# A graph layer on one core: early filter loads into empty tiles, and the four distance products of a pair as one step of TensorE

## The chip, the cores and the metric

The kernel runs on one core of a Trainium2 chip. TensorE (PE in the profile) multiplies matrices, with weight loads listed apart (PEld); VectorE (DVE), ScalarE (ACT) and GpSimd (POOL) work on elements; SyncE (SP) issues most DMAs. SBUF is the memory on the core, PSUM the accumulator banks that TensorE writes. The metric is the device time of one launch, in microseconds.

## What is computed

The input `x` is (64, 256, 256): 64 graphs of 256 nodes with 256 features; `adj` is a 0/1 matrix per graph. Everything is float32. Cut to what matters:

```python
h = maximum(layernorm(x), 0)
# branch 1: two convolutions along the nodes, 1 tap and 17 taps
c = relu(bn1(conv1d(h.T, conv1_w)))
x_conv = relu(bn2(conv1d(c, conv2_w, pad=8)) + h.T).T
# branch 2: messages weighted by distance in a space of 3 numbers
s = h @ w_se.T + b_se                        # (64, 256, 3)
dist = sq[:, :, None] + sq[:, None, :] - 2 * s @ s.T   # sq = sum(s * s)
A = exp(-dist) * adj
x_nmp = A @ relu(h @ w_msg.T + b_msg)
# a GRU cell on both
gi = concat([x_conv, x_nmp]) @ w_ih.T + b_ih
gh = h @ w_hh.T + b_hh
r, z = sigmoid(gi_r + gh_r), sigmoid(gi_z + gh_z)
n = tanh(gi_n + r * gh_n)
out = x + (1 - z) * n + z * h
```

## The kernel before

**Tiling.** Two graphs make a pair (index `i`, 32 pairs), four pairs make a batch (index `b`, 8 batches). The 17-tap convolution is done for a whole batch in a transformed domain. VectorE makes the transform of the input, TensorE multiplies each of 16 bins with that bin's transformed filters, VectorE transforms back (`branch_back` to `p_back`). Each bin has up to three filter matrices ("kinds"), 47 in all, each 128x2x256 numbers (256 KB). They are computed once at the start (`filter_steps`), written to DRAM tensors `filt`, and fetched again for every batch.

**Filters in a batch.** `pending` is the list of filters still to be fetched, `free` the list of free slots. There are nine slots in SBUF (`wb`). `load_kinds` (L902) takes a slot from `free` and a filter from `pending` and issues the DMA on SP. `product` (L927) multiplies with the filter at the head, puts its slot back into `free` and calls `load_kinds`. `begin(m)` (L938) does the first kind of two bins into an accumulator tile `acc` and has ScalarE copy it to the tile's second bank; `complete(m)` (L945) adds the other kinds. Between the transforms of two batches the same nine slots serve the GRU: `roles` (L1071) names them, and `give` (L1077) returns them. Seven are returned at the end of a batch, the last two (`tz0`, `tz1`) inside the next.

**A pair.** `message` computes the messages and the three numbers `s`, `embed` transposes these into `zT`. `affinity` (L1018) computes the distances: for each graph and half, four times in all, a product of nine rows from `zT`, at rows 0, 32, 64 and 96, into one of four PSUM banks (`aux`, a ring), then the exponential on ScalarE, then the multiplication with `adj` on VectorE. `aggregate` multiplies with the messages into a tile `xnm` (a ring of two). `gates` (L1178) does the GRU of a pair with a seven-product scheme: `seven` (L1152) opens two `acc` tiles and one `aux` bank, and calls sums on VectorE (`wb` tiles named by role, weights `w_x`, `w_ih`, `w_hh`). `finish` and `deliver` bring the result out. From the fifth pair on, rows of `adj` and of `h` are turned by transposing DMAs: `load_adj` (L630) fetches turned rows into `adjh` by four DMAs, `join_adj` (L640) is ScalarE's two copies from `adjh` to the tile that VectorE reads.

**What sets the order.** The code doesn't issue instructions. `Recorder` takes each call as a task with an engine, an assumed cost and its dependences (`record`, L334); `plan` (L388) is a list scheduler that simulates the engines with these costs, with TensorE's tasks due in the order of the recording, and `emit` (L463) issues all tasks in the planned order. Each engine then works through its list in order, and waits where an operand isn't there. Almost everything after the first batch's start is one plan. All instructions are issued by one line of `record`, so the profile shows L371 for nearly all; the tile names tell them apart. In the profile, `V`, `U`, `Sv`, `PT` hold transforms, `Yv` the transformed-back result.

The end of a batch, where the next batch's filters are asked for, and the two slots returned inside it, read:

```python
        if b + 1 < NB:
            pending.extend(TURNS)

        def between():
            join_adj(nxt)
        gates(i + 3, between)
        message(nxt)
        if b == NB - 1:
            finish(NP - 1)
        give("axn", "axc", "ah")
        give("bh", "bxn", "bxc", "e")
        load_kinds()
```

## Time and profile before

| | us |
|---|---|
| median of 3 runs (lowest to highest) | 1692.25 (1688.8 to 1693.15) |
| profiled execution, its own time | 1694.44 |
| span in that profile | 1692.7 |
| TensorE busy | 1662.7 |
| VectorE busy | 1458.6 |
| ScalarE busy | 1133.6 |
| GpSimd busy | 227.9 |
| TensorE waiting for filter DMAs, whole span | 5.3 |
| matmuls of the distance products: instructions, busy | 256, 31.0 |

The profile is of one execution. An engine's busy time says how much it did, not whether it set the end; the chain that ended last and the waits of TensorE say that. A wait `A <- B` in the view of waits means that engine A stood idle until B had finished; a wait for several things is put down to the one that came last. In the timeline each line is a start, a length, an engine, an operation with its tiles as out<-in, and a count; the tile's buffer numbers are left out. A float32 matmul appears as two MATMUL instructions.

### The profile page before, as it was taken

Reading aid. Unit: us, or ns where it says so; the run is one execution under the profiler, and the core shown is the slowest. Engines: PE = TensorE matmul, PEld = TensorE weight load, DVE = VectorE, ACT = ScalarE, POOL = GpSimd, SP = SyncE. Lnnn points to the kernel's source line nnn. Section 1 sums busy time; section 2 is a strip of 40 time slices with the busy share of each in tenths; the row PEclk is TensorE's granted clock in tenths of the full one; section 3 lists DMA queues with packets and bytes.
Section 4 is the critical chain, followed back from the end, with each engine's and each line's share of the span. In section 5 each row is a group of like instructions: output and inputs, shape, how many; then the busy total and the mean of one; then the engine's idle time right before and its main releaser. Section 6 shows DMA issues by size and latency. Waiting matters only on the chain.

```text
span 1692.7 us, 26271 instructions
## 1 busy us (share of the span) xinstructions
PE 1662.7 (98%) x8984; PEld 1420.2 (84%) x8984; DVE 1458.6 (86%) x3401; ACT 1133.6 (67%) x2029; POOL 227.9 (13%) x245
## 2 busy tenths in 40 slices
PE   9999999999999999999999999999999999999997
PEld 6888878988889788888889887898888978898886
DVE  7978989798898998898988988979988989789545
ACT  5545776686767767677665877578576776667554
POOL 4211010022010121102110031002211022000010
PEclk9999999999999999999999999999999999999999
DMA  9981566856568365784458645684646846376032
GB/s 240 304 275 61 128 123 160 276 138 128 111 199 235 94 131 112 229 210 97 116 119 270 166 97 117 159 270 111 142 109 204 225 100 131 82 237 144 13 58 55
DMA packets 314936, 261.37 MB, mean 154 GB/s; under 512 B 192875, under 2 KB 240263, under 8 KB 314802
## 3 DMA queue, kind: packets, MB, share of 16 engines
q1 hardware_dynamic: 297010, 216.71, 48.5%
q0 software_dynamic: 17376, 42.66, 11.2%
q8 instruction: 71, 1.16, 0.3%
q14 instruction: 63, 0.52, 0.1%
q10 hardware_dynamic: 416, 0.32, 0.1%
HBM read 156.60 MB, written 43.78 MB: 118 GB/s over the span
## 4 chain that ended last, share of the span: by engine, by line
PE 64%; DVE 29%; DMA 4%; issue 2%; ACT 2%; SPq 0%; DVEq 0%; ACTq 0%
PE acc L371 44%; PE aux L371 20%; DVE V L371 6%; DVE T L371 4%; DVE tr L371 4%; DVE U L371 3%; DVE wb L371 3%; DMA wb<-filt 3%; DVE gn L371 2%; DVE acc L371 2%; DVE Yv L371 1%; DVE PT L371 1%; DVE st L371 1%; DVE msg L371 1%; DMA hh<-halves 1%
## 5 line engine op out<-in xcount | busy, mean ns | idle before, releaser
L371 PE MATMUL acc<-wb,w_ih 128*128 128x256 f32 x768 | 191.9, 379 | 0.0
L371 PEld LDWEIGHTS acc<-wb,w_ih 128*128 128x128 f32 x768 | 146.0, 190 | 19.7
L371 POOL DMA_DIRECT2D back<-in_x_dram x62 | 56.8, 1056 | 750.8 <-ACT back L371 717.5
L371 POOL TENSOR_TENSOR rstd<-rstd,neg_half 128x4 f32<-128x4 f32 x32 | 84.8, 2650 | 455.4 <-DVE shift L371 266.4
L371 PE MATMUL aux<-wb,w_x 128*128 128x256 f32 x576 | 139.9, 384 | 2.5 <-ACT e L371 2.3
L371 PE MATMUL acc<-wb,w_x 128*128 128x256 f32 x576 | 136.2, 382 | 5.3 <-DVE acc L371 5.3
L371 DVE SCALAR_TENSOR_TENSOR V<-T,V 128x128 f32<-128x128 f32 (+2 forms) x448 | 139.9, 372 | 0.0
L371 ACT COPY back<-tr 128x512 uint16<-128x512 uint16 x124 | 128.0, 1077 | 15.2 <-DVE tr L371 14.9
L371 PEld LDWEIGHTS acc<-wb,w_x 128*128 128x128 f32 x576 | 108.0, 190 | 30.5 <-DVE acc L371 12.3
L371 PEld LDWEIGHTS aux<-wb,w_x 128*128 128x128 f32 x576 | 108.8, 191 | 22.1 <-ACT e L371 4.3
L371 PE MATMUL aux<-w_msg,hT 128*128 128x259 f32 x512 | 121.5, 381 | 0.0
L371 PEld LDWEIGHTS acc<-U,wb 128*128 128x128 f32 x1024 | 117.1, 192 | 2.9 <-DMA wb<-filt 1.1
L371 PE MATMUL acc<-U,wb 128*128 128x128 f32 x1024 | 117.6, 275 | 1.6 <-DMA wb<-filt 0.9
L371 PE MATMUL acc<-V,wb 128*128 128x128 f32 x1024 | 118.6, 275 | 0.0
L371 PEld LDWEIGHTS acc<-V,wb 128*128 128x128 f32 x1024 | 116.4, 192 | 0.7 <-DMA wb<-filt 0.3
L371 PE MATMUL acc<-wb,w_hh 128*128 128x256 f32 x384 | 110.1, 381 | 0.7 <-ACT acc L371 0.7
L371 ACT ACTIVATE gn<-acc,bn_columns 128x512 f32<-128x512 f32 (+1 forms) x64 | 43.5, 680 | 97.2 <-PE acc L371 85.6
L371 PEld LDWEIGHTS aux<-w_msg,hT 128*128 128x128 f32 x512 | 96.5, 190 | 14.2
L371 PE MATMUL acc<-Yv,w_ih 128*128 128x256 f32 x380 | 107.9, 379 | 0.1
L371 PE MATMUL aux<-hT,w_c 128*128 128x512 f32 x224 | 105.5, 593 | 0.8 <-DVE msg L371 0.8
L371 PE MATMUL aux<-e,msg 128*128 128x256 f32 x448 | 103.6, 380 | 0.0
L371 PE MATMUL acc<-hT,w_hh 128*128 128x256 f32 x380 | 103.5, 381 | 0.0
(196 smaller groups left out, 3885.6 us busy)
## 6 DMA issues: line engine op xcount, KB each, us to landing
wb<-filt SPq DMA_DIRECT2D x376, 256.0 KB
back<-in_x_dram POOLq DMA_DIRECT2D x62, 256.0 KB, 5.4
out_dram<-back POOLq DMA_DIRECT2D x62, 256.0 KB, 2.8
x<-in_x_dram SPq DMA_DIRECT2D x58, 256.0 KB
halves_d<-halves SPq DMA_DIRECT2D x28, 512.0 KB
adjh<-halves_d SPq DMA_DIRECT2D x112, 128.0 KB
hh<-halves SPq DMA_DIRECT2D x108, 128.0 KB
filt<-Yv SPq DMA_DIRECT2D x18, 224.0 KB
```

Of the source, the lines that this page charges most:

```text
L371: self.tasks.append(Task(engine, lambda: method(*args, **kw), cost, size, self.first))
```

## The change

Four things are different.

- `affinity` takes its four `aux` banks first, then records its four products as one task of TensorE (`joined`): the scheduler can put nothing between them. The four exponentials follow. A task now holds a list of calls, and `emit` makes all of them.
- The assumed cost of such a small product in the scheduler is 0.155 instead of 0.23. The costs of a joined task are added.
- In the last `between` of each batch but the last, after `join_adj(nxt)`, four further slots are added: two in `adjh`, whose content has just been copied, and two in the `xnm` tile that isn't in use. `load_kinds` is called at once, so four filters of the next batch are asked for before the gates of the last pair end.
- `product` doesn't return these four slots to `free`; they serve once per batch.

Since one plan orders everything, a changed task or cost can also move instructions elsewhere. In the built program the orders of all five engines differ in places; the instructions are the same but for the two tiles that four filters in each of seven batches go to.

```diff
@@ record
-                cost = 0.23
+                cost = 0.155
...
-        k = len(self.tasks)
-        self.tasks.append(Task(engine, lambda: method(*args, **kw), cost, size, self.first))
+        if self.joined is not None and engine == "tensor":
+            k = self.joined
+            if k == len(self.tasks):
+                self.tasks.append(Task(engine, [], 0.0, 0, self.first))
+            self.tasks[k].call.append(lambda: method(*args, **kw))
+            self.tasks[k].cost += cost
+        else:
+            k = len(self.tasks)
+            self.tasks.append(Task(engine, [lambda: method(*args, **kw)], cost, size, self.first))
@@ emit
-            self.tasks[k].call()
+            for call in self.tasks[k].call:
+                call()
@@ product
-        free.append(k)
+        if k < SLOTS:
+            free.append(k)
         load_kinds(2)
@@ affinity
-        for g in range(G):
-            for c in range(MC):
-                q = g * MC + c
-                p = aux()
-                rows_q = slice(q * Q, q * Q + KD)
-                mm(p[:, :N], ZT[rows_q, :P], ZT[rows_q, P:], start=True, stop=True)
-                nc.scalar.activation(e_tile[:, g, c], p[:, :N], AF.Exp, scale=-1.0)
+        ps = [aux() for _ in range(G * MC)]
+        nc.joined = len(nc.tasks)
+        for q, p in enumerate(ps):
+            rows_q = slice(q * Q, q * Q + KD)
+            mm(p[:, :N], ZT[rows_q, :P], ZT[rows_q, P:], start=True, stop=True)
+        nc.joined = None
+        for q, p in enumerate(ps):
+            nc.scalar.activation(e_tile[:, q // MC, q % MC], p[:, :N], AF.Exp, scale=-1.0)
@@ end of a batch
         def between():
             join_adj(nxt)
+            if b + 1 < NB:
+                spare = [adjh.bitcast(FP).rearrange("p a n -> p (a n)").rearrange("p (k c d) -> p k c d", k=2, c=DC)[:, k]
+                         for k in range(2)]
+                t = xnms.tiles[(xnms.n + 1) % 2].rearrange("p c (k d) -> p (c k) d", d=D)
+                spare += [t[:, k * DC:(k + 1) * DC] for k in range(2)]
+                slots[SLOTS:] = spare
+                free.extend(range(SLOTS, SLOTS + len(spare)))
+                load_kinds()
         gates(i + 3, between)
```

## Prediction

> **What bounds the kernel now.** First the page: busy shares and the chain that ended last.

> ```profile
> span 1692.7 us, 26271 instructions
> ...
> PE 1662.7 (98%) x8984; PEld 1420.2 (84%) x8984; DVE 1458.6 (86%) x3401; ACT 1133.6 (67%) x2029; POOL 227.9 (13%) x245
> ...
> PE acc L371 44%; PE aux L371 20%; DVE V L371 6%; DVE T L371 4%; DVE tr L371 4%; DVE U L371 3%; DVE wb L371 3%; DMA wb<-filt 3%; DVE gn L371 2%; DVE acc L371 2%; DVE Yv L371 1%; DVE PT L371 1%; DVE st L371 1%; DVE msg L371 1%; DMA hh<-halves 1%
> ```

> TensorE is busy 98% of the span and carries most of the chain. Only work taken off TensorE, or a wait or a slow clock on TensorE itself, can move the end. Next, the products that read zT (the distances), in the timeline of TensorE; columns are start, length, instruction and count. A float32 matmul is two instructions here.

> ```profile
> 135.56 0.69 PE L371 MATMUL aux<-zT 9*128 9x256 f32 x2
> 136.18 0.49 PE L371 MATMUL acc<-PT,wb 128*128 128x128 f32 x2
> 136.60 0.69 PE L371 MATMUL aux<-zT 9*128 9x256 f32 x2
> 137.22 0.49 PE L371 MATMUL acc<-PT,wb 128*128 128x128 f32 x2
> 137.64 0.69 PE L371 MATMUL aux<-zT 9*128 9x256 f32 x2
> 138.26 0.61 PE L371 MATMUL acc<-PT,wb 128*128 128x128 f32 x2
> 138.80 1.22 PE L371 MATMUL aux<-zT 9*128 9x256 f32 x2
> ...
> 910.28 0.71 PE L371 MATMUL aux<-zT 9*128 9x256 f32 x8
> ```

> One product alone holds TensorE 0.62 us (135.56 to 136.18); four in a row take 0.65 us together (910.28 to the next matmul at 910.93). Going through all 32 pairs of graphs, 27 already have the four in a row. Five don't: the pairs at 89.2 and 135.6 (one by one), at 303.6/309.8 and 563.4/570.2 (in two parts) and at 1558.4 to 1570.0 (in three or four). Third, windows of TensorE's clock (columns as on the page; the tenth figure is the granted clock):

> ```profile
> 138.50:145.33 6.83, 6.83 (x29) 5.96 (x29) 3.99 (x8) 2.81 (x6) 1.13 (x2) 0.50 0.24 77
> 145.40:152.00 6.60, 6.60 (x36) 5.90 (x35) 4.88 (x12) 3.91 (x9) 0.00 (x0) 1.00 0.00 0
> ...
> 1561.86:1565.27 3.41, 3.41 (x9) 2.45 (x8) 3.26 (x8) 1.69 (x5) 0.45 (x1) 0.50 0.22 82
> ```

> Twice after the start-up the clock is halved, both times just behind distance products that stand apart. Fourth, the waits of TensorE from 296 to 1520 us, and the start of one batch of the transform in the timeline:

> ```profile
> PE acc L371 <- DMA wb<-filt: 4.4, 7, 1.3
> PE acc L371 <- DVE acc L371: 3.3, 6, 1.1
> PE aux L371 <- ACT e L371: 2.3, 5, 0.5
> ...
> 1092.13 8.40 SPq L371 DMA_DIRECT2D wb<-filt  x10
> 1095.83 1.05 PE L371 MATMUL acc<-Sv,wb 128*128 128x128 f32 x8
> 1098.13 2.94 PE L371 MATMUL acc<-Sv,wb 128*128 128x128 f32 x24 [1.25 <-DMA wb<-filt]
> ```

> The filters of a batch are issued only 4 to 5 us before its first product, since their slots hold the sums of the last gates until then; TensorE did two filters and stood 1.25 us for the third.

> [...] The four products use rows from 0, 32, 64 and 96[...]: 0.65 us for four against 0.62 for one. [...] Here 256 KB took 2.8 to 5.8 us from issue to last arrival at the start of a batch (arrival of each transfer's semaphore in the trace, batch at 892 us).

> **The change, part by part.** The sum is made against the profiled execution: 1694.44 us, 1.74 more than its span.

> 1. Joined products. In 27 pairs nothing changes on TensorE. At 89.2 and 135.6: 4 x 0.62 = 2.50 becomes 0.65, -1.85 each. At 303.6 and 563.4: 0.63 + 0.63 becomes 0.65, -0.62 each. At the end: the stall before 1558.43 stays in another guise, since the next matmul needs Yv, which ScalarE delivers at 1559.7; the third and fourth products (0.62 each) and the 0.68 us wait before the third, less 0.65 for the joined step: -1.3. Sum -6.2. The joined step asks for all four aux banks at once; at 89.2 the last of the four was emptied at 88.8 (ScalarE's copy of taps 88.24 + 0.58), so no wait there. Behind the step on TensorE stand products that don't need its result; the four exponentials take 1.21 us in a row on ScalarE (910.97), as they already do in 27 pairs.

> 2. The clock. If the scattered products caused the two half-clock stretches, joining them removes 6.83/2 = 3.4 and 3.41/2 = 1.7 us. No grouped step is followed by one. Between 0 and 5.1; I take 4.3: the first whole, half of the second, because a TensorE stall of about 2 us for Yv remains there.

> 3. Early filters. In each of seven batches four filter loads (256 KB) go into adjh and the idle xnm tile during the gates before; the first four products find them in place, and the seven slots that come free at the old moment serve products 5 to 11, 3.6 us later (four products of 0.9 us). The waits above sum to 4.4 us. Of these 1.0 (at 896.75) has a second cause: ScalarE's copy out of the accumulator ended at 896.52. So -3.5; between 0 and -5, the latter if waits put down to ScalarE's zT (0.7) are filters too. The order of the built program shows these loads on SP ahead of the last transposes, among the hh loads.

> 4. What moves. The adjacency rows (4 x 128 KB) that stood before the batch now follow it on SP: two behind the eleventh filter, two behind the 33rd, and wait for the first products to free adjh. In the trace of before the 33rd filter was issued at 920.16, 28 us into the batch; transfers around it took 3 to 6 us. The ScalarE copy that needs them is put behind the accumulator copy of the fifth pair of bins (925.46 before), so it may start late by at most 0.5 us; behind it stands the copy at 927.25, whose reader on TensorE comes after eight w_msg products that end at 934.2. Hidden by about 5 us; without that cover 1.4 us a batch. SP's transpose of hh (4.2 us of issue) stands behind the two loads and comes 1.3 us later; it landed at 926.75 and its next reader was issued at 931.13. GpSimd only swaps a small multiply with a load.

> 5. New order. The list is replanned with 0.155 us a product (joined 0.62, measured 0.65) where it had 0.23. In the gates one or two w_x products move from before a distance step to behind it. The stall there (0.4 us, for e's bank) turns into one for VectorE's sum in acc, due at the same time (971.38 against 971.40 in the trace): nothing. VectorE is 91 to 93% busy in the gates, so not every microsecond taken off TensorE is kept. No row prices that: between 0 and 8 us; I take 2.5.

> Sum: -6.2 - 4.3 - 3.5 + 2.5 = -11.5: the profiled execution would take 1683. The median of the runs shown, 1692.25, is 2.2 below the profiled one, so I predict 1692.25 - 11.5 = 1681 for the median.

> **Rivals.**

> - *Little but the joining counts.* The products were together in 27 of 32 pairs, the clock falls again elsewhere, and the first product of a batch is held by the accumulator anyway (896.52 above). Then -6.2 with 1 to 2 us given back: about 1687.5. Against it: at 1098.13 no accumulator was waited for.
> - *All of it is kept.* Both clock stretches and all filter waits go, nothing is given back: -6.2 - 5.1 - 5 = -16.3: 1676. For it: TensorE has only 30 us idle, and VectorE waits on TensorE more often than the reverse.
> - *Slower: the late adjacency rows.* SP issues in order, and ScalarE works in order: if the second pair of rows lands more than about 10 us after its issue at some 920.6, ScalarE's copy holds the accumulator copy past 934 and TensorE stands. To end 0.3% slower than before it must eat the other gains of 11.5 and 5.1 more, 16.6/7 = 2.4 us a batch, so it decides from a landing some 12 us after issue: about 1698. Against it: transfers there took 3 to 6 us, and the queue has room (261 GB/s over that stretch of 50 us, while the first filters landed 0.65 us apart, some 400).

> **How the numbers follow.** 0.3% (5.1 us) is about what a measurement of this kernel can tell from no change. Forecast, 1677 to 1687: 0.55. All kept: 0.13, faster too. Joining alone: 0.20, of which 0.12 is below 1687.2 and 0.08 within the bound. Late rows or another new stall of that size: 0.12, of which 0.10 slower. So faster 0.80, same 0.10, slower 0.10. Range 1673 to 1691: the low end takes all gains with some reserve, the high end joining alone with its gain mostly given back.

> **What would show it.** Right: 32 groups of eight zT instructions, no half clock at 138 and 1562, waits of TensorE for filters from 4.4 us to below 1, the first four filters landed before a batch starts. Wrong: waits of ScalarE for adjh or of TensorE for its copies inside the batch; waits for acc from VectorE that grow from 3.3 us to 10 or more; half clock in a new place.

## The result, and the profile after

The changed kernel took 1670.33 us in the median (1669.41 to 1671.88), the kernel before 1692.13 (1688.8 to 1693.15): a ratio of 0.9877 [0.9861, 0.9893]. That is 21.8 us less, about twice the forecast 11.5 us and below the range of 1673 to 1691. Its profiled execution took 1671.88 us, with a span of 1670.1. First its page: span, busy shares, and the chain that ended last.

```profile
span 1670.1 us, 26281 instructions
...
PE 1645.7 (99%) x8984; PEld 1413.3 (85%) x8984; DVE 1456.8 (87%) x3401; ACT 1127.2 (67%) x2029; POOL 236.0 (14%) x245
...
PE acc L378 49%; PE aux L378 21%; DVE V L378 5%; DVE tr L378 3%; DVE U L378 3%; DVE T L378 3%; DVE wb L378 3%; DVE acc L378 2%; DVE gn L378 2%; DMA wb<-filt 2%; DVE st L378 1%; DVE PT L378 1%; DVE msg L378 1%; PE aux L374 1%; DVE Sv L378 0%
```

TensorE's busy time fell by 17 us and its share of the chain rose; VectorE does what it did, ScalarE's busy time fell by 6 us and GpSimd's rose by 8. (Lines are shifted: what was L371 is L378; the joined products are issued by L374.) Next the second pair's distance products in TensorE's timeline, where four stood apart before, and the clock of that place, 128.1 to 141.7 us, in windows.

```profile
132.36 0.71 PE L374 MATMUL aux<-zT 9*128 9x256 f32 x8
133.01 2.05 PE L378 MATMUL acc<-PT,wb 128*128 128x128 f32 x16
```

```profile
128.10:134.90 6.80, 6.80 (x65) 6.35 (x63) 6.80 (x13) 5.62 (x19) 0.00 (x0) 1.00 0.32 111
134.90:141.70 6.80, 6.80 (x44) 6.24 (x43) 6.66 (x16) 5.29 (x12) 1.12 (x2) 1.00 0.29 77
```

All eight instructions take 0.65 us (132.36 to 133.01), and the clock stays at 1.00 where it was 0.50 from 138.50 us on before. Third, TensorE's waits from 280 to 1520 us; this one line is the whole answer:

```profile
PE acc L378 <- DVE acc L378: 5.8, 12, 0.5
```

In these seven batches the waits for filters and for ScalarE are gone, and what remains is 12 times half a microsecond behind a distance step in the gates. (In the first batch, which gets no early filters, TensorE still waits 2.4 us for them, 0.9 before.) Last, the start of a batch in the timeline (TensorE, and SP's queue):

```profile
875.81 4.29 SPq L378 DMA_DIRECT2D wb<-filt  x7
...
879.51 0.60 PE L378 MATMUL aux<-w_msg,hT 128*128 128x259 f32 x2
879.95 1.95 PE L378 MATMUL acc<-Sv,adjh 128*128 128x128 f32 x16
880.81 1.47 SPq L378 DMA_DIRECT2D adjh<-halves_d  x2
881.73 1.95 PE L378 MATMUL acc<-Sv,xnm 128*128 128x128 f32 x16
883.52 0.72 PE L378 MATMUL acc<-V,wb 128*128 128x128 f32 x5
```

The first four products read their filters from adjh and xnm, and follow the last product of the messages without a gap. The seven filters issued at the old moment, from 4.1 us ahead, aren't needed until 883.52.

To place the gain, the span is cut around the products that use the filters. A transform stage runs from the start of the matmul ahead of a batch's first such product to the start of the matmul behind its last. The forecast column gives the prediction's terms in the stage where they belong (us):

| part of the span | before | after | change | forecast |
|---|---|---|---|---|
| up to the first transform stage | 71.5 | 69.9 | -1.6 | 0 |
| first batch's transform stage | 74.66 | 67.17 | -7.5 | -7.1 |
| the seven later transform stages | 368.65 | 358.90 | **-9.75** | -4.1 |
| the seven stretches of gates between | 1031.6 | 1029.0 | -2.6 | +1.9 |
| the last batch's gates, to the end | 146.3 | 145.1 | -1.1 | -2.2 |

The first batch came out near its forecast (a second profile of the changed kernel has 65.29 us there; it waits 0.4 us for filters in that batch where this one waits 2.4). The later transform stages gained more than twice as much as forecast, and the gates gave nothing back: 5.6 and 4.5 of the 11 us by which the forecast fell short.

### The profile page after: what moved, and what is told of

The parts are those of the page before. It is cut to its first block, busy times and chain, and to the rows that moved or that the text cites. A ratio compares the mean times of both kernels' runs of the same rounds, so it can differ in the third digit from the quotient of the medians.

```text
span 1670.1 us, 26281 instructions
## 1 busy us (share of the span) xinstructions
PE 1645.7 (99%) x8984; PEld 1413.3 (85%) x8984; DVE 1456.8 (87%) x3401; ACT 1127.2 (67%) x2029; POOL 236.0 (14%) x245
## 4 chain that ended last, share of the span: by engine, by line
PE 70%; DVE 24%; DMA 3%; issue 2%; ACT 1%; SPq 0%; DVEq 0%; ACTq 0%
PE acc L378 49%; PE aux L378 21%; DVE V L378 5%; DVE tr L378 3%; DVE U L378 3%; DVE T L378 3%; DVE wb L378 3%; DVE acc L378 2%; DVE gn L378 2%; DMA wb<-filt 2%; DVE st L378 1%; DVE PT L378 1%; DVE msg L378 1%; PE aux L374 1%; DVE Sv L378 0%
## 5 line engine op out<-in xcount | busy, mean ns | idle before, releaser
L378 PE MATMUL acc<-wb,w_ih 128*128 128x256 f32 x768 | 191.9, 379 | 0.0
L378 PEld LDWEIGHTS acc<-wb,w_ih 128*128 128x128 f32 x768 | 145.9, 190 | 19.8
L378 POOL DMA_DIRECT2D back<-in_x_dram x62 | 56.5, 1051 | 727.7 <-ACT back L378 379.5
L378 POOL TENSOR_TENSOR rstd<-rstd,neg_half 128x4 f32<-128x4 f32 x32 | 85.8, 2682 | 458.5 <-DVE shift L378 272.5
L378 PE MATMUL acc<-wb,w_x 128*128 128x256 f32 x576 | 136.9, 383 | 7.8 <-DVE acc L378 7.8
L378 ACT COPY back<-tr 128x512 uint16<-128x512 uint16 x124 | 128.3, 1078 | 22.5 <-DVE tr L378 22.2
L378 DVE SCALAR_TENSOR_TENSOR V<-T,V 128x128 f32<-128x128 f32 (+2 forms) x448 | 141.1, 379 | 0.0
L378 PE MATMUL aux<-wb,w_x 128*128 128x256 f32 x576 | 138.1, 382 | 0.0
L378 PEld LDWEIGHTS acc<-wb,w_x 128*128 128x128 f32 x576 | 106.9, 190 | 36.3 <-DVE acc L378 17.7
L378 PEld LDWEIGHTS aux<-wb,w_x 128*128 128x128 f32 x576 | 108.7, 191 | 17.3 <-DVE wb L378 2.6
L378 PE MATMUL aux<-w_msg,hT 128*128 128x259 f32 x512 | 121.7, 381 | 0.0
L378 PE MATMUL acc<-V,wb 128*128 128x128 f32 x1024 | 118.5, 275 | 0.8 <-DMA wb<-filt 0.8
L378 PEld LDWEIGHTS acc<-U,wb 128*128 128x128 f32 x1024 | 116.9, 192 | 2.6 <-ACT acc L378 1.7
L378 PE MATMUL acc<-U,wb 128*128 128x128 f32 x1024 | 117.2, 275 | 1.6 <-DMA wb<-filt 1.6
L378 PEld LDWEIGHTS acc<-V,wb 128*128 128x128 f32 x1024 | 116.4, 192 | 1.3 <-DMA wb<-filt 1.2
L378 ACT ACTIVATE gn<-acc,bn_columns 128x512 f32<-128x512 f32 (+1 forms) x64 | 43.5, 680 | 106.6 <-PE acc L378 101.5
L378 PE MATMUL acc<-Yv,w_ih 128*128 128x256 f32 x380 | 108.4, 381 | 2.1 <-ACT Yv L378 2.1
L378 PE MATMUL acc<-wb,w_hh 128*128 128x256 f32 x384 | 109.4, 380 | 0.7 <-ACT acc L378 0.7
L378 PEld LDWEIGHTS aux<-w_msg,hT 128*128 128x128 f32 x512 | 96.5, 190 | 14.3
L378 ACT COPY back<-gn 128x1024 uint16<-128x1024 uint16 x62 | 82.8, 1342 | 36.3 <-DMA gn<-back 36.3
L378 PE MATMUL aux<-hT,w_c 128*128 128x512 f32 x224 | 106.1, 592 | 0.0
L378 PE MATMUL acc<-hT,w_hh 128*128 128x256 f32 x380 | 104.0, 380 | 0.0
```

Of the source, the lines that this page charges most:

```text
L378: self.tasks.append(Task(engine, [lambda: method(*args, **kw)], cost, size, self.first))
```

## The experiments

**The early filters undone, and alone.** The first takes them out of the changed kernel, the second does them alone. The runs are spread over three chips, on which the kernel before took 1689.71, 1692.2 and 1692.96 us in the median; between chips, the ratios to it are what can be compared.

```diff
@@ without the early filters
-        if k < SLOTS:
-            free.append(k)
+        free.append(k)
@@ the last between of a batch
         def between():
             join_adj(nxt)
-            if b + 1 < NB:
...
-                load_kinds()
@@ the early filters alone: affinity and record as before, and
-                cost = 0.155
+                cost = 0.23
```

> The joined step and the new cost, without the early filter loads. Theory A (every stall of TensorE at the start of a batch in the kernel before, 7.8 us over seven batches, was a wait for filters, also those put down to ScalarE): these stalls come back, 1670.3 + 7.8 = about 1678; waits for wb<-filt are seen again at each batch start. Rival B (as predicted: filters were worth 3.5 us, since the accumulator was late as well; the surplus came from the new order): about 1674.

> The kernel before plus the early filter loads alone; distance products not joined, cost 0.23. Theory A: 1692.1 - 7.8 = about 1684, no stall of TensorE over 0.3 us at the start of a batch, the copy of the accumulator by ScalarE included. Rival B: about 1688.5, and a stall of some 1 us at batch starts that ends with ScalarE's copy. Both: the products of the first two pairs stay apart, so a half clock near 138 us is seen again if it comes from them.

Without them: 1681.4 us, ratio 0.995 [0.9935, 0.9965]. Alone: 1678.85 us, ratio 0.9942 [0.9927, 0.9958]. Both theories had put the early filters too low. They are worth 0.6% alone and 0.7 to 0.8% on top of the rest, some 10 to 13 us; the two parts alone, 0.5% and 0.58%, add up to most of the 1.23%. Without them the seven later transform stages take 367.3 us, 8.4 more than in the changed kernel; with them alone 359.0, nearly the changed kernel's 358.9. (In this plan the pair that was split near 303.6 happens to be whole, which is 0.6 us of it.) The gates between take 1031.9 us without the early filters, 2.9 more than in the changed kernel, with 3.1 us of new waits of TensorE for VectorE's wb and e; why those come was not traced.

**The assumed cost.** The new cost alone; and the kernel without early filters again, with the old cost.

```diff
@@ the cost alone: the kernel before, with
-                cost = 0.23
+                cost = 0.155
@@ the old cost: the kernel without the early filters, with
-                cost = 0.155
+                cost = 0.23
```

> The kernel before with the assumed cost 0.155 alone. In the built order 13 pairs then have their four products in two or more parts, where it was 5. Theory A (a new cost alone gives nothing; what counts is that the four stand together): eight more pairs at 0.62 us, about 1697. Rival B (the surplus came from planning with a truer cost): 1687 or less.

> Joined distance products with the old assumed cost (0.23) and without the early filters. It differs from the run with joining and the new cost (1681.4 us, 0.995 of before) in the assumed cost alone. Theory A (the assumed cost by itself is worth little once the products are joined): 0.994 to 0.996, within 2 us of that run. Theory B (the run with the cost alone was 3.3 us faster than before because the truer cost makes the better plan): 0.997 to 0.998, some 3 us slower than that run. Both expect waits of TensorE for filters of 2.5 us or more from 280 to 1520 us.

The cost alone: 1686.42 us, ratio 0.998 [0.9972, 0.9987], faster although it splits the products of 9 of the 32 pairs in the profile (13 were expected), where 5 were split before. A was wrong, and B's 1687 of 1692, a ratio of 0.997, isn't quite reached. Joining with the old cost: 1682.29 us, ratio 0.9942 [0.9922, 0.9962], no different from joining with the new one (0.995). So once the products are joined, no effect of the cost is seen; one of 0.1 or 0.2% would not show here. In the run with the cost alone the seven later stages take 363.7 us, 5 less than before, without any early filter: how long a batch's start waits for its filters depends on the plan too. Why this plan waits less wasn't traced. Early filters still stand out: leaving aside three runs below that add work to every pair, the six profiles with them have 358.9 to 359.9 us in these stages, and the five without them 362.9 to 368.65.

**How many, and how early.** Three runs beside each other on one chip: the changed kernel again; only the two filters in adjh early; and the same four spare slots, but all eleven filters asked for at the old moment.

```diff
@@ two early
                 spare = [adjh ... for k in range(2)]
-                t = xnms.tiles[(xnms.n + 1) % 2].rearrange("p c (k d) -> p (c k) d", d=D)
-                spare += [t[:, k * DC:(k + 1) * DC] for k in range(2)]
@@ spare slots at the old moment
         give("bh", "bxn", "bxc", "e")
-        load_kinds()
+        if b + 1 < NB:
+            spare = [...]
+            slots[SLOTS:] = spare
+            free.extend(range(SLOTS, SLOTS + len(spare)))
+        load_kinds(SLOTS + 4)
```

> The changed kernel once more, so that the others of this group can be compared with it on one chip. Expected about 0.988 of the kernel before (1670 us if that takes 1692); transform stages of the seven later batches 51.27 us each, no wait of TensorE for filters from 280 to 1520 us.

> The changed kernel with only two early filters a batch (those in adjh), not four. The two early ones serve begin(0); the filters of begin(2) come at the old moment. Theory A (a batch's start needs the first two in place, the others then have 1.8 us more than before): the changed kernel plus 0 to 2 us, transform stages of the later batches 51.3 to 51.6 us each. Theory B (all four are needed, because the waits of begin(2), 3.6 us in the trace of before, are waits of their own): plus 4 to 6 us, stages 52.0 to 52.3 us each.

> The changed kernel with the same four spare slots, but asked for at the old moment together with the seven returned ones: the first seven filters go to the returned slots, the next four to the spare ones. It has more slots and nothing early. Theory A (it is the early issue that counts): the waits at a batch's start return, 7.8 us in all in the trace of before, so the changed kernel plus 6 to 9 us, stages 52.1 to 52.6 us each. Theory B (it is the number of slots, a deeper queue of filters, that counts): the changed kernel plus 0 to 2 us.

The changed kernel: 1670.24 us, ratio 0.9873 [0.9852, 0.9894]. Two early: 1671.68, 1.4 more, and the seven stages 359.9 against 359.1: A. Spare slots at the old moment: 1674.12, 3.9 more, between the two theories, with 362.9 us for the seven stages. TensorE's waits for filters from 280 to 1520 us, first in the run without early filters and with the old cost, then with the spare slots at the old moment:

```profile
PE acc L378 <- DMA wb<-filt: 4.3, 7, 1.5
```

```profile
PE acc L378 <- DMA wb<-filt: 2.3, 4, 0.9
```

One of those four, in TensorE's timeline of the run with spare slots at the old moment:

```profile
284.14 3.26 PE L378 MATMUL acc<-Sv,wb 128*128 128x128 f32 x24
288.32 1.16 PE L378 MATMUL acc<-Sv,wb 128*128 128x128 f32 x8 [0.91 <-DMA wb<-filt]
```

The stalls in the first 5 us of a batch, here behind three products, are back. Those about 12 us into a batch (`begin(2)`), which the two joined kernels without early filters show in four and in three of the seven batches, stay away: with more slots the filters of `begin(2)` are asked for earlier. So in these stages about half of the 8.4 us comes with the additional slots and the other half with asking early. In the whole time the slots weigh more: on this chip the median goes from 1682.29 us (joined, old cost, neither slots nor early filters) to 1674.12 with the slots and to 1670.24 with both, 8.2 and 3.9 us.

**The clock.** The changed kernel with the first two pairs apart again:

```diff
@@ affinity
+        if i < 2:
+            for q in range(G * MC):
+                p = aux()
+                rows_q = slice(q * Q, q * Q + KD)
+                mm(p[:, :N], ZT[rows_q, :P], ZT[rows_q, P:], start=True, stop=True)
+                nc.scalar.activation(e_tile[:, q // MC, q % MC], p[:, :N], AF.Exp, scale=-1.0)
+        else:
```

> The changed kernel, but the products of the first two pairs recorded one by one; the rest of the order is nearly the same. Theory A (the thin products standing apart halve the clock): 2 x 1.85 for the products and 3.4 for a half clock of 6.8 us behind the second pair near 135 us, about 1677.4. Rival B (the half clock at 138 us was chance[...]): 1674, no half clock there.

1675.74 us, ratio 0.9924 [0.9911, 0.9936]: against the changed kernel's 0.9873 to 0.9877 some 8 us are lost, nearer to A. The first transform stage takes 72.35 us (67.17 and 65.29 in two profiles of the changed kernel), and the half clock is back, for one stretch of 3.41 us where A had 6.8:

```profile
132.69:136.10 3.41, 3.41 (x14) 1.96 (x14) 2.19 (x6) 1.60 (x4) 0.43 (x1) 1.00 0.24 87
136.10:139.52 3.42, 3.42 (x16) 3.00 (x15) 2.79 (x7) 1.46 (x3) 0.70 (x2) 0.50 0.32 93
```

Such a stretch stands just behind the second pair in all four profiles in which the first two pairs are apart (before, early filters alone, the cost alone, this one), and in none of the six others up to here.

Within each profile the starts of all half clock stretches lie whole multiples of 3.413 us apart; that is the length of a single one in the traces. In before, ahead of the end, they are at 12.21, 138.50 and 1561.86 us, 37 and 417 such lengths apart. I cut each of the ten profiles up to here into windows of this length, counted from those starts, and added up TensorE's idle time and the time of nine-row products in every window from 60 us on to 25 us ahead of the end; a product's time runs here to the start of the next matmul. The highest sum ahead of full clock and the lowest ahead of half clock were 1.45 and 1.87 us in before, 1.34 and 2.09 us in the profile of the changed kernel shown above, and 1.80 and 1.87 us over all ten. There is one exception: the second of the two halved windows at 138.5 us of before follows a window with 1.15 us, itself at half clock. And the stretch at 12.21 us of before, outside the time counted, follows a window with 1.74 us of idle time (8.80 to 12.21). These are sums of this kernel's traces and no more. To test whether such products bring on half clock by themselves, three runs put additional products ahead of each of the 32 joined steps, and a fourth tried to use the finding:

```diff
@@ affinity, ahead of the four products, in the same task
+        for _ in range(4):                 # one at a time
+            mm(ps[0][:, :N], ZT[:KD, :P], ZT[:KD, P:], start=True, stop=True)
@@ or
+        for _ in range(4):                 # four at a time
+            for q, p in enumerate(ps):
+                rows_q = slice(q * Q, q * Q + KD)
+                mm(p[:, :N], ZT[rows_q, :P], ZT[rows_q, P:], start=True, stop=True)
@@ or
+        for _ in range(6):                 # 128 rows
+            mm(ps[0][:, :N], w_msg[:, 0, :P], w_msg[:, 0, :N], start=True, stop=True)
@@ embed of the last pair but one, behind the transposes (the attempt)
+            for _ in range(3):
+                mm(p[:, 2 * P:], w_msg[:, 0, :P], w_msg[:, 0, :N], start=True, stop=True)
```

> The changed kernel with four additional nine-row products, one after the other on the same rows (0.62 us each, 2.5 us together), ahead of every joined step; their results are overwritten by the step. Theory A (nine-row products count as idle for the clock): each of the 32 pairs has 3.1 us of them in a row, and in about 4 of 5 more than 1.87 us fall into one window; so 20 to 30 half clock stretches between 80 and 1620 us, and a time of 1670 + 32 x 2.5 + 25 x 1.7 = about 1790 us. Theory B (a busy TensorE is full, and the stretches of before had another cause): 0 to 2 stretches and about 1750 us.

> The changed kernel with four additional rounds of all four products ahead of every joined step (16 more nine-row products, 4 x 0.65 = 2.6 us); their results are overwritten. Theory A (what counts is that TensorE runs nine-row products, whether one or four at a time): 20 to 30 half clock stretches and about 1670 + 83 + 42 = 1795 us. Theory B[...]: 0 to 2 stretches and about 1753 us; then grouping the products helps the clock for more than their shortness.

> The control: the changed kernel with six additional products of 128 rows (0.43 us each, 2.6 us) ahead of every joined step instead of the nine-row ones; their results are overwritten. Both theories: no half clock stretch other than near the stall for Yv of the last batch and at the end, and about 1670 + 32 x 2.6 = 1753 us. Half clock stretches in numbers here would mean that it is the delay of the other engines behind the step, and not the thin products, that lowers the clock.

Each was measured in one execution. One at a time: 1738.62 us and 14 half clock stretches behind distance steps. Four at a time: 1717.72 us and none. With 128 rows: 1746.18 us and none. (Each of the three also has the one behind the stall for Yv, and one at the end.) A step now takes 2.35 us one at a time and 2.37 four at a time, so for TensorE the two differ in the clock alone as far as the profiles show, and 14 stretches cost 20.9 us, 1.5 each. Here is one step of the first run, in the timeline and in the windows, and one of the second:

```profile
1401.70 2.42 PE L374 MATMUL aux<-zT 9*128 9x256 f32 x16
```

```profile
1401.09:1404.50 3.41, 3.41 (x22) 2.48 (x21) 2.12 (x5) 1.06 (x3) 0.00 (x0) 1.00 0.00 0
1404.50:1407.91 3.41, 3.41 (x10) 2.70 (x9) 3.29 (x10) 2.07 (x5) 0.00 (x0) 0.50 0.00 0
```

```profile
711.53 2.44 PE L374 MATMUL aux<-zT 9*128 9x256 f32 x40
```

```profile
711.09:714.50 3.41, 3.41 (x50) 2.87 (x49) 2.95 (x5) 2.91 (x6) 0.00 (x0) 1.00 0.77 257
714.50:717.92 3.42, 3.42 (x34) 3.42 (x33) 2.13 (x5) 2.02 (x6) 0.00 (x0) 1.00 0.46 138
```

Both first windows are busy throughout (3.41 of 3.41 us) and hold a whole step. Half clock thus came behind nine-row products one at a time although TensorE shows no idle time there; it came behind none of the steps with the same products four at a time on different rows, and behind none with the delay alone, from products of 128 rows. So A holds for the first run, with fewer stretches than its 20 to 30, and B for the second. The additional products took 0.43 us each, not 0.62, so a step holds some 1.9 us of single ones (2.35 less 0.43 for its joined part). The figures of the ten profiles don't carry over exactly: the 14 windows ahead of half clock hold 2.21 to 2.35 us of a step, and three with 2.23 to 2.31 us stayed at full clock. So what tells these windows apart isn't settled.

> The changed kernel with three additional float32 products of 128 rows (0.43 us each, into an unused half of a bank) put into TensorE's stall of 2.1 us for Yv near 1536 us in the last batch. Nothing waits for them. Theory A (a window of 3.41 us of TensorE's clock is followed by half clock when idle time and nine-row products together fill more than about 1.85 us of it; in ten profiles the windows below 1.84 us were followed by full clock and those above 1.87 us by half): the stall shrinks to about 0.8 us, no half clock there, whatever the position of the window; 0 to 1.7 us less than the changed kernel in an execution, so a ratio of 0.986 to 0.988 to before. Theory B (the half clock there has another cause): half clock at about 1538 us as in four of five profiles of kernels with joined products and this stall.

The attempt: 1671.99 us, ratio 0.9875 [0.9855, 0.9895], no gain. "Nothing waits for them" was wrong, as the timeline of TensorE and ScalarE shows:

```profile
1534.95 1.46 PE L374 MATMUL aux<-w_msg 128*128 128x256 f32 x6
1536.50 1.25 ACT L378 COPY zT<-aux 128x128 f32<-128x128 f32 x5 [1.30 <-PE aux L374]
1537.78 1.33 ACT L378 ACTIVATE Yv<-Yv,bn_shift 128x512 f32<-128x512 f32 x2
1538.55 2.07 PE L378 MATMUL acc<-Yv,w_ih 128*128 128x256 f32 x4 [2.14 <-ACT Yv L378]
```

ScalarE's copies out of that bank waited for the last additional product, and Yv stands behind them on ScalarE. The stall was as long as before, and half clock followed; this run doesn't tell A from B. The earlier profiles with joined products speak for A. Five of these seven (not four of five) have the half clock there, and in them the window ahead holds 2.09 us of the stall; in the two without it a boundary leaves 1.80 and 1.45 us at most in one window. A version that beats the changed kernel wasn't found.

## Why the prediction was wrong

**The step that failed is 3, the early filters,** and by its size: -3.5 was forecast, and with it at most -5. The later transform stages gained 9.75 us, of which 0.6 are the joined products of the pair at 303.6. Undoing the early filters alone brings 8.4 us back into these stages, and by the ratios some 12 us into the whole time. Two things were mis-sized.

First, I took only the waits that the view of waits puts down to filters, 4.4 us. In the first 3 us of a batch and again some 12 us into it (`begin(0)`, `begin(2)`) the trace of before has 7.8 us of stalls on TensorE. Another 1.4 us were named after ScalarE's zT, xnm and gn, and 2.0 us were short or put down to issue. With the early filters alone all but 0.3 us are gone, so they were waits for filters under another name.

Second, I subtracted 1.0 us at 896.75 for "a second cause". These are the weight load and the matmul of that wait in the timeline of before:

```profile
896.72 3.43 PEld L371 LDWEIGHTS acc<-Sv,wb 128*128 128x128 f32 x30 [1.37 <-ACT xnm L371]
```

```profile
896.75 3.47 PE L371 MATMUL acc<-Sv,wb 128*128 128x128 f32 x29 [0.99 <-DMA wb<-filt]
```

The weight load's wait is named after ScalarE's copy, which ended at 896.52. But by the order of the ring that copy freed the other accumulator tile, which is needed only in `begin(1)`; the first one was free at 895.23. The filter that the first product reads was sent second; it landed at 896.61, 1.3 us after the one sent first, and that ended the wait. The rest of the stages' gain, some 1.3 us, lies in the same place: if the matmuls of a stage are laid beside those of the changed kernel one by one, about 9 us of delay stand in the first 17 us of the seven batches, and none later.

**Step 5, the new order,** failed as well, by 4.5 us: with it the gates were forecast 1.9 us longer (2.5 given back to VectorE, less 0.6 for a joined pair). The gates took 2.6 us less, and run at 146.6 to 146.9 us in six of seven batches. TensorE's waits for VectorE's sum in acc grew from 3.3 to 5.8 us, but the waits for e (2.3 us) and msg (0.8) went. That one stall would turn into the other was right; a further loss for VectorE's load had no row behind it. What shortens the gates isn't isolated: the two joined runs without additional slots took 1031.9 and 1030.7 us there, nearly what before did, the runs with such slots 1028.2 to 1029.8, the cost alone 1028.6.

**Step 1, the joined products,** is right: 32 groups of eight instructions, together 28.6 us from first start to the next matmul, against 35.7, with 6.8 and 6.6 us of waits in these sums. That is 7.2 us for the forecast 6.2. The two early pairs and the first clock stretch (3.7 and 3.4 us by forecast) are in the first stage's -7.5.

**Step 2, the clock,** is right for the first stretch. The second moved from 1562 to 1538.5, behind the stall for Yv, as I had half allowed for; a half clock in a new place was one of the signs of being wrong. In a second profile of the changed kernel it is absent, though the stall is the same. The windows around it, first in the profile with half clock, then in the one without:

```profile
1535.09:1538.50 3.41, 1.32 (x7) 0.93 (x7) 3.41 (x8) 3.31 (x12) 0.97 (x2) 1.00 0.92 127
1538.50:1541.91 3.41, 3.41 (x10) 2.38 (x9) 3.41 (x8) 2.03 (x7) 0.57 (x1) 0.50 0.56 180
```

```profile
1530.63:1534.05 3.42, 2.48 (x12) 1.72 (x10) 3.42 (x8) 2.49 (x10) 1.80 (x2) 1.00 0.54 90
1534.05:1537.46 3.41, 1.96 (x8) 1.35 (x8) 3.41 (x9) 3.24 (x9) 0.96 (x2) 1.00 0.82 165
1537.46:1540.87 3.41, 3.41 (x17) 2.96 (x16) 3.41 (x8) 0.62 (x2) 0.18 (x1) 1.00 0.23 82
```

The stall takes 2.09 us in both. In the first it lies whole in one window (busy 1.32 of 3.41), in the second a boundary cuts it in two (2.48 and 1.96). That products standing apart cause the half clock was a conjecture of mine, from two places in the trace of before. The runs bear it out for nine-row products one at a time (14 stretches behind the steps) and speak against it for four at a time (none).

**Step 4, what moves,** is right: the two pairs of adjacency rows issued from 880.81 and 903.0 on had landed at 885.2 and 908.2, ScalarE waited 0.4 us for such rows over 1240 us, and TensorE for none of it. The slow rival needed a landing 12 us after issue; each of these took 3.5 to 4.5.

The rival "all of it is kept" came nearest, at 1676, but it too stopped at 5 us for the filters. The gain of 1.6 us ahead of the first transform stage is luck and no step's doing: in the profile of before a half clock lay there, from 12.2 to 15.6 us, and in no other profile, those of the early filters alone and of the cost alone included.

## What to carry to other kernels

Before pricing a prefetch, add up every stall of the bottleneck engine at the place where the data is first used, whatever name the wait has, and compare with a place where the same instructions run without a gap; named waits were 56% of it here (4.4 of 7.8 us). Ask of a "second cause" whether the waiting instruction itself reads or writes that tile. Asking earlier and having more slots are two gains; here the slots brought half in the transform stages and two thirds in all. And products of nine rows were better done side by side than one by one, for the clock (1717.72 against 1738.62 us in the runs with products added) as well as for their own time (four in 0.65 us against 0.62 for one alone).
